# A seven-bank PSUM ring as one tensor, with two neighbouring banks read by one instruction

## Chip, cores and metric

The kernel runs on one core of a Trainium2 chip. The metric is the device time in microseconds (us) of one execution. The kernel before took 1364.9 us (median of three runs, 1364.61 to 1367.81). The profiled execution took 1365.17 us, and its span, from the first to the last instruction, is 1363.4 us.

## What is computed

One decoder layer in fp32 on x of shape (4, 1024, 256) with a context of shape (4, 64, 256): self-attention, cross-attention and a ternary feed-forward, each behind a layer norm and added to x.

```python
x = x + attn(layernorm(x), W_qkv, b_qkv, W_out, b_out)       # 16 heads of 16, softmax(q k) / 16
x = x + xattn(layernorm(x), ctx, Wq, bq, Wk, bk, Wv, bv, Wo, bo)
x = x + ffn(layernorm(x), W_fc, ln_w, ln_b, W_proj)          # 256 -> 1024 -> 256, gelu, layernorm
```

Self-attention is most of the work: 4 batches x 16 heads x 1024 x 1024 scores, which are computed twice, once to find the row maxima and once, transposed, to take the exponential.

## The kernel before

**Units and steps.** The scores are worked in 16 units `u` (a batch and a group of four heads, two pairs of two). A unit has 16 steps (`half`, `kb`): a block of 128 keys against 512 queries, in the loop at lines 891 to 956. There are thus 256 steps. In each step TensorE gets, in program order (`ordered` at lines 54 to 63 fixes the order of TensorE and of the DMA queue, not that of the readers):

1. `scores(..., 0)` (L872): a product for each of two heads into two banks of PSUM, then a second product that subtracts the maxima (`sel`, `mT`). The two heads sit in the two halves of TensorE's rows, so the products of a pair run side by side. ScalarE then takes Exp of each bank (L888).
2. `top()`: the next piece of `maxima` (L412) for the unit after: two more banks of scores, which VectorE reduces to a row maximum, one bank at a time (L433).
3. Perhaps a filler ("rows": a turning of blocks by TensorE transposes into two banks, or a piece of cross-attention in two banks).
4. `scores(..., 1)`: two banks. 5. `top()`: two banks.
6. `weigh` (L796): the exponentials of the step before, times the values, into the one bank `ps_acc`.
7. Perhaps fillers ("cols": a projection or the like, one bank each).

**The ring.** PSUM has eight banks here, of 512 fp32 columns in 128 partitions. One is `ps_acc`; seven are a pool `ps_ring` (L175), handed out in turn by `bank()` (L183), so the n-th allocation gets the bank of the (n-7)-th. The first product into a bank waits for the instruction that last read it. `two_banks()` (L186) hands out two banks in a row. The fillers are chosen in `fill` (L692) by credits and due times when the program is built; nothing of that choice depends on how a bank is read.

**Readers of two banks.** Besides L433 and L888, two banks are filled together and read by two instructions in `turned` (L200: the copies at L269, L307, L451 and L604, and the reciprocal and product of `normalised`, L298 and L299), at L592 (maxima of cross-attention) and at L625 (its exponentials). After the last unit the ring is closed (L962) and the feed-forward runs with two other pools, `ps_wide` and `ps_misc`, which the change does not touch in size.

Of the kernel before, what the change touches and what calls it, by code (L numbers as in the profile page):

```python
# [30 lines left out]
def decoder_layer(ctx, tc, a, out):  # L31
# [23 lines left out]

    def matmul(*args, **kwargs):
        ordered(nc.tensor.matmul(*args, **kwargs))  # L57

    def transpose(*args):
        ordered(nc.tensor.transpose(*args))  # L60
# [68 lines left out]
    nc.vector.memset(eps_t, LN_EPS)  # L129
# [45 lines left out]
    open_psum("ring", 7, [P, 512])  # L175
# [10 lines left out]
    def two_banks():  # L186
        return [bank() for _ in range(2)]
# [12 lines left out]
    def turned(blocks):  # L200


        n = len(blocks)
        sides = 2 if state["split"] else 1
        w = P // sides
        banks = [bank() for _ in range(sides)]
        for i, block in enumerate(blocks):
            for r, pt in enumerate(banks):
                side = slice(w * r, w * r + w)
                transpose(pt[:, i * w : (i + 1) * w], block[side, :], ident[side, side])  # L210
        return [pt[:, 0 : n * w].rearrange("p (b i) -> p b i", i=w) for pt in banks]

    def turned_tokens(copy, src, n):


        step = min(n, 4) if state["split"] else 2
        for k0 in range(0, n, step):
            sides = turned([src(c, k0 + k) for c in range(2) for k in range(step)])
            for r, v in enumerate(sides):
                copy(  # L220
                    slice(k0 * P, (k0 + step) * P), r, len(sides),
                    v.rearrange("p (c k) i -> p c k i", c=2),
                )

    def of_side(dst, r, sides):

        return dst.rearrange("p c (k r i) -> p r c k i", r=sides, i=P // sides)[:, r, :, :, :]

    def ln_stats(pool, mv, blocks):

        for i, t in blocks:
            st = pool.tile([P, 6], F32, tag="bn", name="bn", bufs=3)
            nc.vector.bn_stats(out=st, in_=xs(t)[:, 0, :])  # L233
            nc.vector.bn_aggr(out=mv[:, i, :], in_=st)

    def ln_rstd(pool, rs, mv):
        n = mv.shape[1]
        sd = pool.tile([P, n], F32, tag="sd", name="sd", bufs=2)
        nc.scalar.activation(sd, mv[:, :, 1], AF.Sqrt, bias=eps_t[:, 0:1])
        nc.vector.reciprocal(out=rs, in_=sd)  # L240

    def ln_normalised(pool, mv, rs, i, t, n):
        xn = pool.tile([P, n, E], F32, tag="xn", name="xn", bufs=2)
        if state["split"]:
            nmr = pool.tile([P, n], F32, tag="nmr", name="nmr", bufs=2)
            nc.vector.scalar_tensor_tensor(
                nmr, mv[:, i : i + n, 0], -1.0, rs[:, i : i + n], ALU.mult, ALU.mult
            )
            for k in range(n):
                nc.scalar.activation(  # L250
                    xn[:, k, :], xs(t + k)[:, 0, :], AF.Identity, bias=nmr[:, k : k + 1],
                    scale=rs[:, i + k : i + k + 1],
                )
            return xn
        for k in range(n):
            nc.vector.tensor_scalar(  # L256
# [5 lines left out]
    def ln_transposed(dst, xn, rest=None):  # L262

        def copy(tokens, r, sides, v):
            to = of_side(dst[:, :, tokens], r, sides)
            nc.scalar.copy(to, v)  # L269
            if rest is not None:  # L270
                nc.vector.tensor_tensor(  # L271
                    of_side(rest[:, :, tokens], r, sides), v, to.bitcast(F32), ALU.subtract
                )

        turned_tokens(copy, lambda c, k: xn[:, k, c * P : (c + 1) * P], xn.shape[1])
# [9 lines left out]
    def head_proj(dst, w, bias, g, src, cols):  # L285
        pq = bank()[:, 0 : cols.stop - cols.start]
        product(pq, [(w[:, c, g * P : (g + 1) * P], src[:, c, cols]) for c in range(2)])
        nc.scalar.activation(dst[:, cols], pq, AF.Identity, bias=bias[:, g : g + 1])

    def normalised(dst, acc_sb):  # L290


        views = turned([acc_sb[:, n * P : (n + 1) * P] for n in range(4)])
        n = NG // len(views)
        for side, v in enumerate(views):
            heads = v.rearrange("p t (j e) -> p t j e", e=32)
            r = post_pool.tile([P, 4, n, 1], F32, tag="r", name="r", bufs=3)
            nc.vector.reciprocal(out=r, in_=heads[:, :, :, 0:1])  # L298
            nc.vector.tensor_tensor(  # L299
                dst[:, :, side * n : (side + 1) * n, :], heads[:, :, :, 1 : 1 + D],  # L300
                r.to_broadcast([P, 4, n, D]), ALU.mult,
            )

    def transposed_blocks(src, n):
        t = post_pool.tile([P, 2, n * P], F32, tag="ao", name="ao")
        turned_tokens(
            lambda tokens, r, sides, v: nc.scalar.copy(of_side(t[:, :, tokens], r, sides), v), src, n  # L307
        )
        return t

    def out_proj(ao, k, n, w, t):
# [5 lines left out]
        nc.vector.tensor_tensor(  # L317
# [23 lines left out]
    def project(b, c):  # L341
# [6 lines left out]
        for side, half in ((0, 0), (1, 0), (1, 1), (0, 1)):  # L348
# [3 lines left out]
            for i0 in range(0, 512, width):  # L352
# [6 lines left out]
                nc.scalar.activation(hl[:, 0, part].bitcast(F32R), pq, AF.Identity, bias=bias)  # L359
                nc.vector.scalar_tensor_tensor(  # L360
# [40 lines left out]
    def values(b):  # L401
        for i in range(NT):
# [4 lines left out]
            nc.scalar.copy(  # L407
# [4 lines left out]
    def maxima(u):  # L412
# [4 lines left out]
        for half in range(2):  # L417
# [4 lines left out]
            for t, pair in order:  # L422
                q, k = qk_of[u][pair]
                for kh in range(2):
                    sides = two_banks()
# [6 lines left out]
                    for n, pm in enumerate(sides):  # L432
                        nc.vector.tensor_reduce(  # L433
                            mx[:, t, 2 * pair + n : 2 * pair + n + 1, kh], pm, AX.X, ALU.max
# [5 lines left out]
    def turn_maxima(u, mx):  # L440
        nm = main.tile([P, 4, NG], F32, tag="nm", name="nm", bufs=2)
        nc.vector.tensor_reduce(nm, mx, AX.X, ALU.max, negate=True)
        by_side = nm.rearrange("p t (a n) -> p t n a", a=2)
        dst = nm_s[:, :, :, 0:2, :]
        nc.vector.tensor_copy(dst[:, :, :, :, 0].bitcast(F32R), by_side)
        nc.vector.tensor_tensor(dst[:, :, :, :, 1], by_side, dst[:, :, :, :, 0], ALU.subtract)
        yield
        views = turned([nm_s[:, n, :, :, :].rearrange("p n a l -> p (n a l)") for n in range(4)])
        mT = main.tile([P, 512], F32R, tag="mT", name="mT", bufs=3)
        for r, v in enumerate(views):  # L450
            nc.scalar.copy(mT.rearrange("p (k r i) -> p r k i", r=len(views), k=4)[:, r, :, :], v)  # L451
# [27 lines left out]
    def context():  # L479
# [9 lines left out]
        nc.vector.tensor_reduce(own, ident.rearrange("p (s j i) -> p j s i", s=2, j=4), AX.XY, ALU.add)  # L489
        one = post_pool.tile([P, 32], F32, tag="one", name="one")  # L490
        nc.vector.tensor_reduce(one, ident.rearrange("p (s h l) -> p h s l", s=2, l=2), AX.XY, ALU.add)
        nc.vector.tensor_copy(
            sel_x, one[:, 0:8].rearrange("p (h o) -> p h o", o=1).to_broadcast([P, 8, SK])
        )
        for c in range(2):
# [5 lines left out]
            for j in range(4):  # L501
                nc.vector.tensor_scalar(
# [3 lines left out]
        for b in range(B):  # L506
# [9 lines left out]
            for n in range(2):  # L516
                r = slice(64 * n, 64 * n + 64)
                nc.vector.tensor_tensor(
# [5 lines left out]
    def value_bias():  # L524
# [10 lines left out]
        nc.vector.scalar_tensor_tensor(bo, pt, 1.0 / 16.0, bo, ALU.mult, ALU.add)  # L535
# [4 lines left out]
    def post(b):  # L540
# [25 lines left out]
        for half in range(2):  # L566
# [6 lines left out]
            ln_transposed(xnT, xn)  # L573
# [7 lines left out]
            for t in range(4):  # L581
                yield "rows"
                pm = two_banks()
# [7 lines left out]
                for s in range(2):  # L591
                    nc.vector.tensor_reduce(  # L592
                        nm[:, t, s, :], pm[s].rearrange("p (h k) -> p h k", k=SK), AX.X, ALU.max,
# [4 lines left out]
            nc.vector.tensor_copy(dst[:, :, :, :, 0].bitcast(F32R), nm)  # L598
            nc.vector.tensor_tensor(dst[:, :, :, :, 1], nm, dst[:, :, :, :, 0], ALU.subtract)
            yield "rows"  # L600
            views = turned([nm_x[:, t, :, :, :].rearrange("p s h l -> p (s h l)") for t in range(4)])
            mT = post_pool.tile([P, 512], F32R, tag="mTx", name="mTx")
            for r, v in enumerate(views):
                nc.scalar.copy(mT.rearrange("p (k r i) -> p r k i", r=len(views), k=4)[:, r, :, :], v)  # L604
            att = post_pool.tile([P, 4, NG, NG * D], F32, tag="attx", name="attx")
            before = None
            for g in range(NG):
                yield "rows+" if g else "rows"
                pe = two_banks()
# [14 lines left out]
                for p in range(2):  # L624
                    nc.scalar.activation(ex[:, p, :], pe[p], AF.Exp, scale=0.25)  # L625
# [11 lines left out]
                nc.scalar.copy(oT, pa)  # L637
# [84 lines left out]
    def ternary(name, *shape):  # L722
# [13 lines left out]
        for i, cols in enumerate(parts):  # L736
            yield "free"
            nc.vector.tensor_reduce(
# [3 lines left out]
        nc.vector.memset(ones, 1.0)  # L742
# [4 lines left out]
        nc.vector.tensor_reduce(thr[:, 0:1], pt[:, 0 : len(parts)], AX.X, ALU.add)  # L747
        nc.vector.tensor_scalar(thr[:, 0:1], thr[:, 0:1], 1.0 / (P * n), GAMMA_EPS, ALU.mult, ALU.add)
        nc.vector.tensor_scalar(thr[:, 1:2], thr[:, 0:1], -0.5, None, ALU.mult)
        nc.vector.tensor_scalar(thr[:, 0:1], thr[:, 0:1], 0.5, None, ALU.mult)  # L750
        for cols in parts:
            yield "free"
            neg = main.tile([P, 512], F32, tag="hl", name="neg", bufs=2)
            nc.vector.tensor_scalar(neg, flat[:, cols], thr[:, 1:2], None, ALU.is_lt)
            nc.vector.scalar_tensor_tensor(
# [4 lines left out]
    def bias_row():  # L760
# [10 lines left out]
        nc.vector.tensor_copy(yrow, pt[:, 0:E])  # L771
# [24 lines left out]
    def weigh(u, half, kb, exps, acc):  # L796
# [11 lines left out]
        nc.scalar.copy(oT, acc)  # L808
# [27 lines left out]
    for pair in range(2):  # L836

        for n in range(2):
            c = 64 * n + 2 * pair
            for i in range(2):  # L840
                nc.vector.tensor_tensor(
                    sel_f[:, pair, :], sel_f[:, pair, :], ident[:, c + i : c + i + 1].to_broadcast([P, P]), ALU.add
                )
    nc.vector.tensor_copy(sel, sel_f)
# [27 lines left out]
    def scores(u, half, kb, pair):  # L872

        q, k = qk_of[u][pair]
        pe = two_banks()
# [11 lines left out]
        for n in range(2):  # L887
            nc.scalar.activation(ex[:, n, :], pe[n], AF.Exp)  # L888
# [74 lines left out]
    main_stack.close()  # L963
    open_psum("wide", 2, [P, 2, 512])
# [11 lines left out]
    def widen(i):  # L976
# [3 lines left out]
        for t in range(0, NH, 2):  # L980
            cols = slice(t * P, (t + 2) * P)
            xn = ln_normalised(ffn, mv3, rs3, t0 + t, t0 + t, 2)
            ln_transposed(xh[:, :, cols], xn, rest=xl[:, :, cols])
# [7 lines left out]
        for t in range(NH):  # L991
# [9 lines left out]
            nc.scalar.activation(h[:, t, :], ph.rearrange("p a f -> p (a f)"), AF.Gelu)  # L1001
            st = ffn.tile([P, 2, 6], F32, tag="bnh", name="bnh", bufs=3)
            for half in range(2):
                nc.vector.bn_stats(out=st[:, half, :], in_=h[:, t, half * 512 : (half + 1) * 512])  # L1004
            nc.vector.bn_aggr(out=mv[:, t, :], in_=st)
# [3 lines left out]
        nc.vector.scalar_tensor_tensor(nmr, mv[:, :, 0], -1.0, rs, ALU.mult, ALU.mult)  # L1009
        for t in range(0, NH, 2):  # L1010
            yield ""
            nc.vector.tensor_scalar(
                h[:, t, :], h[:, t, :], mv[:, t, 0:1], rs[:, t : t + 1], ALU.subtract, ALU.mult
            )
            nc.scalar.activation(
# [4 lines left out]
    def narrow(i):  # L1020
# [6 lines left out]
        for c in range(HID // P + 2):  # L1027
            if c < HID // P:
# [6 lines left out]
                nc.scalar.activation(hT, pt, AF.Copy, scale=w)  # L1035
                nc.vector.scalar_tensor_tensor(hl, pt, w, hT.bitcast(F32), ALU.mult, ALU.subtract)  # L1036
# [13 lines left out]
        for n in range(2):  # L1050
            rows = xs(t0 + 2 * n, 2)
            nc.vector.tensor_tensor(
# [111 lines left out]
```

## Time and profile before

| view | value |
|---|---|
| time, three runs | 1364.9 us (1364.61 to 1367.81) |
| profiled execution: time, span, mean granted clock | 1365.17 us, 1363.4 us, 0.979 |
| stage with the ring: the 256 steps | from 58 us to 1098 us |
| TensorE busy, 60 to 340 / 340 to 640 / 640 to 1000 us | 267.36 / 294.17 / 352.89 us |
| VectorE busy in the same stretches | 211.24 / 237.91 / 283.13 us |
| ScalarE busy in the same stretches | 191.54 / 214.13 / 252.76 us |
| feed-forward and last cross-attention, 1100 to 1363 us: TensorE, VectorE, ScalarE busy | 235.04 / 170.29 / 157.53 us |

The groups in the profile have the line, engine and operation, what is written and read with partitions x elements, the count, the time that at least one of them was busy, the mean duration of one, and the idle time of the engine before them with what ended it. PE is TensorE's products, PEld its weight loads, DVE is VectorE, ACT ScalarE. All products have line 57 and all transposes line 60, since one helper each records them; what they are is told by the tiles: `ps_ring<-q,k` is a product of `scores`, `ps_ring<-mT,sel` its second product, `ps_ring<-k,q` one of `maxima`, `ps_acc<-exp,v_sb` one of `weigh`.

### The profile page before, as it was taken

How to read it: one execution, taken by the hardware profiler on the slowest of the kernel's cores; microseconds unless marked ns; L12 is line 12 of the kernel's file. 1: busy time of each engine (PE TensorE's matmuls, PEld its weight loads, DVE VectorE, ACT ScalarE, POOL GpSimd, SP SyncE). 2: the span in 40 equal slices, each digit the busy share in tenths (PEclk: the TensorE clock that was granted, in tenths of full speed). 3: DMA queues.
4: the chain of work that ended last, by engine and by line, in shares of the span. 5: the costliest groups of instructions: out<-in, count | busy, mean ns of one | idle time of the engine just before them, and what ended most of it. 6: DMA issues, size and time to landing. Idle time of an engine off the chain costs nothing.

```text
span 1363.4 us, 27651 instructions
## 1 busy us (share of the span) xinstructions
PE 1282.1 (94%) x11000; PEld 717.4 (53%) x11000; DVE 1004.7 (74%) x2110; ACT 898.5 (66%) x1654; POOL 80.0 (6%) x86
## 2 busy tenths in 40 slices
PE   3879999999999999999999999999999988999987
PEld 1434445545545454444545544545455466776777
DVE  4877777867878877877877777878889357565665
ACT  1377666756687667777676676676766746474765
POOL 4000000003010000011000000010000012000000
PEclk9889999999999999989999999999999989999989
DMA  5440312312130202131212112212210010100000
GB/s 169 126 143 30 111 42 68 94 48 63 41 85 1 63 7 57 33 93 31 64 35 60 38 27 75 82 53 73 55 40 1 2 62 1 44 19 31 1 31 32
DMA packets 46064, 72.72 MB, mean 53 GB/s; under 512 B 11280, under 2 KB 27920, under 8 KB 45936
## 3 DMA queue, kind: packets, MB, share of 16 engines
q1 hardware_dynamic: 44720, 68.47, 17.0%
q8 instruction: 87, 1.43, 0.4%
q10 hardware_dynamic: 1072, 2.10, 0.4%
q0 software_dynamic: 144, 0.39, 0.2%
q14 instruction: 41, 0.34, 0.1%
HBM read 46.81 MB, written 24.12 MB: 52 GB/s over the span
## 4 chain that ended last, share of the span: by engine, by line
PE 73%; DVE 16%; ACT 8%; issue 2%; DMA 1%; SPq 0%; DVEq 0%; ACTq 0%
PE ps_ring L57 42%; PE ps_acc L57 15%; PE ps_wide L57 8%; DVE mx L433 8%; PE ps_misc L57 3%; ACT exp L888 3%; PE ps_misc L60 2%; PE ps_ring L60 2%; DVE nm L592 2%; ACT xn L250 1%; DVE xn L256 1%; DVE bn L233 1%; DMA x<-in_x 1%; ACT ex L625 1%; ACT hl L359 1%
## 5 line engine op out<-in xcount | busy, mean ns | idle before, releaser
L433 DVE TENSOR_REDUCE mx<-ps_ring 128x1 f32<-128x512 f32 x1024 | 646.4, 682 | 157.6 <-PE ps_ring L57 156.7
L888 ACT ACTIVATE exp<-ps_ring 128x512 f32<-128x512 f32 x1024 | 549.2, 606 | 191.1 <-PE ps_ring L57 187.5
L57 PE MATMUL ps_ring<-q,k 64*128 64x512 f32 x1024 | 280.5, 474 | 8.0 <-ACT exp L888 5.9
L57 PE MATMUL ps_ring<-k,q 64*128 64x512 f32 x1024 | 260.2, 425 | 20.1 <-DMA q<-kept_q 7.9
L57 PE MATMUL ps_acc<-exp,v_sb 128*32 128x512 f32 x2048 | 275.3, 610 | 0.0
L57 PE MATMUL ps_ring<-mT,sel 64*128 64x512 f32 x1024 | 232.8, 400 | 0.2 <-ACT mT L451 0.2
L57 PEld LDWEIGHTS ps_ring<-q,k 64*128 64x128 f32 x1024 | 115.5, 185 | 198.4 <-ACT exp L888 69.0
L57 PEld LDWEIGHTS ps_ring<-k,q 64*128 64x128 f32 x1024 | 124.2, 186 | 100.2 <-ACT exp L888 41.3
L57 PEld LDWEIGHTS ps_ring<-mT,sel 64*128 64x128 f32 x1024 | 108.0, 186 | 6.3 <-ACT mT L451 0.7
L57 PEld LDWEIGHTS ps_acc<-exp,v_sb 128*32 128x32 f32 x2048 | 40.5, 108 | 67.4 <-issue 65.6
L1004 DVE BATCH_NORM_STATS2 bnh<-h 128x6 f32<-128x512 f32 x64 | 41.2, 679 | 34.1 <-ACT h L1001 34.0
L1001 ACT ACTIVATE h<-ps_wide 128x1024 f32<-128x1024 f32 x32 | 32.7, 1026 | 41.6 <-PE ps_wide L57 41.5
L1036 DVE SCALAR_TENSOR_TENSOR hl<-ps_misc,lnw,hT 128x512 fp32r<-128x512 f32 x64 | 46.4, 733 | 18.2 <-ACT hT L1035 18.2
L57 PE MATMUL ps_wide<-wproj,hl 128*128 128x256 f32 x256 | 46.2, 303 | 12.6 <-DVE hl L1036 12.5
L57 PE MATMUL ps_wide<-wfc,xl 128*128 128x512 f32 x128 | 56.5, 442 | 1.4 <-DVE xl L271 1.4
L57 PE MATMUL ps_wide<-wfc,xh 128*128 128x512 f32 x128 | 54.3, 424 | 0.0
L1035 ACT ACTIVATE hT<-ps_misc,lnw 128x512 fp32r<-128x512 f32 x64 | 42.6, 687 | 16.3 <-PE ps_misc L60 16.3
L233 DVE BATCH_NORM_STATS2 bn<-x 128x6 f32<-128x256 f32 x96 | 38.8, 416 | 8.1 <-DMA x<-in_x 6.4
L57 PEld LDWEIGHTS ps_wide<-wproj,hl 128*128 128x128 f32 x256 | 34.9, 191 | 16.2 <-DVE hl L1036 14.8
L280 POOL TENSOR_TENSOR x<-x,xbo 128x512 f32<-128x512 f32 x16 | 20.6, 1295 | 367.0 <-ACT xn L250 358.5
L57 PE MATMUL ps_wide<-wproj,hT 128*128 128x256 f32 x256 | 41.4, 284 | 0.0
L407 ACT COPY v_sb<-ps_ring 128x256 f32<-128x256 f32 x32 | 12.0, 375 | 41.0 <-PE ps_ring L57 30.6
(166 smaller groups left out, 1467.1 us busy)
## 6 DMA issues: line engine op xcount, KB each, us to landing
k<-kept_k SPq DMA_DIRECT2D x248, 64.0 KB
q<-kept_q SPq DMA_DIRECT2D x240, 64.0 KB
kept_q<-hl SPq DMA_DIRECT2D x15, 512.0 KB
kept_k<-hl SPq DMA_DIRECT2D x14, 512.0 KB
out<-x SPq DMA_DIRECT2D x16, 256.0 KB
x<-in_x SPq DMA_DIRECT2D x3, 1024.0 KB
x_kept<-x SPq DMA_DIRECT2D x3, 1024.0 KB
x<-x_kept SPq DMA_DIRECT2D x3, 1024.0 KB
```

The lines of the kernel that those rows point to most:

```text
L57: ordered(nc.tensor.matmul(*args, **kwargs))
L60: ordered(nc.tensor.transpose(*args))
L233: nc.vector.bn_stats(out=st, in_=xs(t)[:, 0, :])
L250: nc.scalar.activation(xn[:, k, :], xs(t + k)[:, 0, :], AF.Identity, bias=nmr[:, k : k + 1], scale=rs[:, i + k : i + k + 1],)
L280: nc.gpsimd.tensor_tensor(xs(t, 2), xs(t, 2), row.rearrange("p (o d) -> p o d", o=1).to_broadcast([P, 2, E]), ALU.add,)
L433: nc.vector.tensor_reduce(mx[:, t, 2 * pair + n : 2 * pair + n + 1, kh], pm, AX.X, ALU.max)
L592: nc.vector.tensor_reduce(nm[:, t, s, :], pm[s].rearrange("p (h k) -> p h k", k=SK), AX.X, ALU.max, negate=True,)
L888: nc.scalar.activation(ex[:, n, :], pe[n], AF.Exp)
L1001: nc.scalar.activation(h[:, t, :], ph.rearrange("p a f -> p (a f)"), AF.Gelu)
L1004: nc.vector.bn_stats(out=st[:, half, :], in_=h[:, t, half * 512 : (half + 1) * 512])
L1035: nc.scalar.activation(hT, pt, AF.Copy, scale=w)
L1036: nc.vector.scalar_tensor_tensor(hl, pt, w, hT.bitcast(F32), ALU.mult, ALU.subtract)
```

## The change

The seven banks become one tensor `ring` of 128 x 7 x 512, allocated once; `ring_bank()` hands its banks out in the same order as before. As all instructions on it now touch one tensor, each is told by hand which others it need not wait for: an instruction names the span of banks that it touches, and is freed of those that touch other banks only (`by_bank`, called for each instruction of TensorE, VectorE and ScalarE through a thin wrapper). `two_banks()` returns beside the two banks a list of views: one view of both when they are neighbours in the tensor, and two views of one bank each when the first is bank 6 and the second bank 0. The readers loop over the views, so two neighbouring banks are read by one instruction. The order of TensorE's instructions is unchanged.

```diff
+    NB = 7
+    rings = []
+    spans = [(i, i + n) for n in (1, 2) for i in range(NB + 1 - n)]
+    def by_bank(ins, *operands):
...
+                at = ap.offset % (NB * 512)
+                last = at + sum(step * (count - 1) for step, count in ap.ap[1:])
+                mine = at // 512, last // 512 + 1
...
+            for span in spans:
+                if span[1] <= mine[0] or mine[1] <= span[0]:
+                    tc.add_to_no_dep_group(f"not_{span}", ins.ins)
+            tc.declare_no_dep(ins.ins, group=f"not_{mine}", keep=keep, reason="other banks")
...
-    open_psum("ring", 7, [P, 512])
+    ring = ring_pool.tile([P, NB, 512], F32, name="ps_ring")
+    def ring_bank():
+        i = ring_at[0]
+        ring_at[0] = (i + 1) % NB
+        return ring[:, i, :]
...
     def two_banks():
-        return [bank() for _ in range(2)]
+        i = ring_at[0] if state["banks"] == "ring" else NB
+        pair = [bank() for _ in range(2)]
+        if i + 1 < NB:
+            return pair, [(slice(0, 2), ring[:, i : i + 2, :])]
+        return pair, [
+            (slice(n, n + 1), one.rearrange("p (o f) -> p o f", o=1)) for n, one in enumerate(pair)
+        ]
...
-                    for n, pm in enumerate(sides):
-                        nc.vector.tensor_reduce(
-                            mx[:, t, 2 * pair + n : 2 * pair + n + 1, kh], pm, AX.X, ALU.max
+                    for n, v in views:
+                        vector.tensor_reduce(
+                            mx[:, t, 2 * pair + n.start : 2 * pair + n.stop, kh], v, AX.X, ALU.max
                         )
...
-        for n in range(2):
-            nc.scalar.activation(ex[:, n, :], pe[n], AF.Exp)
+        for n, v in views:
+            scalar.activation(ex[:, n, :], v, AF.Exp)
         return ex
```

The same loop over views is put at L269, L307, L451, L604, L298 and L299, L592 and L625. In `normalised` the transposes write their 64 columns as two runs of 32, so that the heads of both banks lie in one regular pattern for the reader.

## Prediction, written before the changed kernel was run

> **What bounds the kernel now.** I read the page first, for busy time and the two big readers of the ring, then the waits, then the timeline of single steps.
>
> ```profile
> PE 1282.1 (94%) x11000; PEld 717.4 (53%) x11000; DVE 1004.7 (74%) x2110; ACT 898.5 (66%) x1654; POOL 80.0 (6%) x86
> ...
> L433 DVE TENSOR_REDUCE mx<-ps_ring 128x1 f32<-128x512 f32 x1024 | 646.4, 682 | 157.6 <-PE ps_ring L57 156.7
> L888 ACT ACTIVATE exp<-ps_ring 128x512 f32<-128x512 f32 x1024 | 549.2, 606 | 191.1 <-PE ps_ring L57 187.5
> ```
>
> TensorE sets the pace; VectorE and ScalarE are idle a quarter and a third of the time, waiting for TensorE's products. But 94% does not mean that TensorE is never held up: its records are modelled, and a product that started late still looks busy. The waits of its weight loads from 60 to 1098 us say more (in total, how many, the longest):
>
> ```profile
> PEld ps_ring L57 <- ACT exp L888: 113.4, 310, 1.7
> ...
> PEld ps_ring L57 <- DVE mx L433: 41.3, 90, 1.6
> ```
>
> 310 loads wait for an Exp and 90 for a maximum: TensorE wants a bank that its last reader has not given back. Which reader of a pair it is, the timeline shows. A step without filler, 2.90 us long (columns: start, length, engine, what, count, idle before and who ended it):
>
> ```profile
> 109.49 0.50 PE L57 MATMUL ps_ring<-q,k 64*128 64x512 f32 x2
> ...
> 110.32 2.07 ACT L888 ACTIVATE exp<-ps_ring 128x512 f32<-128x512 f32 x4 [1.06 <-PE ps_ring L57]
> 110.49 2.48 DVE L433 TENSOR_REDUCE mx<-ps_ring 128x1 f32<-128x512 f32 x4 [0.27 <-PE ps_ring L57]
> ...
> 110.75 0.71 PE L57 MATMUL ps_ring<-k,q 64*128 64x512 f32 x2
> 110.97 0.18 PEld L57 LDWEIGHTS ps_ring<-k,q 64*128 64x128 f32 x1 [0.26 <-ACT exp L888]
> ...
> 111.39 1.06 PE L57 MATMUL ps_acc<-exp,v_sb 128*32 128x512 f32 x8
> 112.39 0.19 PEld L57 LDWEIGHTS ps_ring<-q,k 64*128 64x128 f32 x2 [0.84 <-ACT exp L888]
> ```
>
> Count the banks of this step: scores 0, 1; maxima 2, 3; scores 4, 5; maxima 6, 7. Bank 7 of seven is bank 0 again, which this step's own first Exp reads. That Exp starts at 110.32, ends 0.60 later at 110.92, and the load for the eighth product starts at 110.97. Its partner started at 110.75, so TensorE has lost 0.22 us already, and what follows is late by that.
>
> I counted this over the whole ring, by giving each bank in TensorE's order its last reader and comparing that reader's end with the first load of the bank's next use, seven places on. In 505 places of 2575 the load comes no later than 0.13 us after the reader's end. In 268 of these the reader is the first of a pair, in 184 the second, in 53 a single one; 96 and 95 of the first kind are the second score product or the second maximum behind the first Exp. So the release that TensorE stands and waits for is mostly that of a first bank, which one instruction over both banks delays.
>
> **The change, part by part.** *The readers' cost.* The nearest row to an Exp of 1024 is the Gelu over two banks at L1001, 1026 ns, against 606 ns for the Exp of 512. Four chained Exps take 2.07 us, so a second one adds 0.49 us: the pair ends now 1.09 us after its start, in future 1.03. A maximum takes 682 ns; the additions at L317 take 415 ns for 256 elements and 676 for 512, thus 0.52 us per 512, and a maximum over 1024 about 0.68 + 0.53 = 1.21 us, where the pair ends now after 1.29. Saved per merged pair: 0.06 us of ScalarE, 0.08 of VectorE. Following the bank numbers modulo seven, 1013 of 1190 pairs become one instruction (444 of 512 of Exp, 432 of 512 of maxima); the others straddle banks 6 and 0. That is 27 us of ScalarE and 35 of VectorE, all beside TensorE's work: both engines already wait for products.
>
> Here the Trainium skill speaks for a larger gain: "ScalarE: Activation LUTs", in "What ACT_TABLE_LOAD costs", gives an ACTIVATE 186 ns apart from its elements, and "Advanced Engine Details and Errata", "The Read-Write Bubble", advises 512 or 1024 elements to spread such a cost. With 186 ns the saving would be 83 us of ScalarE; the chain of four shows that most of it overlaps already, and I take 0.06. Either number is off TensorE's path.
>
> *The releases.* The first bank of a merged pair comes back at 1.03 us instead of 0.60 (+0.43) behind an Exp and at 1.21 instead of 0.68 (+0.53) behind a maximum. In the step above: reader 110.32 + 1.03 = 111.35, load at 111.40 instead of 110.97, and `ps_acc` and the next step follow 0.43 later. Nothing hides it: TensorE runs in order, the products behind it wait too, and the wait begins anew in each step from that step's first scores, so it adds up step by step instead of being paid once. The products of the next step find their banks long free (the second pair of Exps ends at about 1.9 + 0.9 us into a step that then lasts 3.3).
>
> A step with turned blocks has ten banks, and the second score product is the one that takes bank 0 again:
>
> ```profile
> 1061.44 1.08 ACT L888 ACTIVATE exp<-ps_ring 128x512 f32<-128x512 f32 x2 [0.45 <-PE ps_ring L57]
> ...
> 1062.09 0.18 PEld L57 LDWEIGHTS ps_ring<-q,k 64*128 64x128 f32 x1 [0.23 <-ACT exp L888]
> ...
> 1062.57 0.19 PEld L57 LDWEIGHTS ps_ring<-k,q 64*128 64x128 f32 x2 [0.19 <-ACT exp L888]
> ...
> 1063.01 1.07 PE L57 MATMUL ps_acc<-exp,v_sb 128*32 128x512 f32 x8
> ```
>
> Now two waits follow each other, on the first Exp (1062.03) and on the second (1062.52). Merged, both banks come at 1062.47: the second score product loads at 1062.52, the second product of that side runs 0.23 later, the last maximum another 0.23 later at 1062.98, when its bank is free as well (this step's maxima start at 1061.68; + 1.21). `ps_acc` starts 0.43 after that, as it does now after 1062.58: 1063.41 instead of 1063.01, +0.40. The same working for a step that turns the maxima (at 610.02 us) gives +0.28; I take +0.36 for the mixture. If the first pair straddles the ring's end, the merged maxima still bind here, so no share is taken off.
>
> With 16 steps of cross-attention's maxima (at 504.84) the same sums give +0.35, and with its exponentials (at 536.23) +0.02, since there the product that takes bank 0 starts at 1.90 us anyway.
>
> *The sum.* I sorted the 256 steps by their order of products:
>
> - 103 with nothing or only column fillers between: 0.43 x 219/256 (the share of first score pairs that are neighbours) x 103 = 38 us
> - 84 with one turning: 0.36 x 84 = 30 us
> - 24 with cross-attention's maxima: 8 us; 10 with two turnings, at the same 0.35: 4 us; 22 with its exponentials: under 1 us
> - 13 odd ones: not costed
>
> Together +80 us in 1040 us of steps. Against it stands about 1 us before the first step, where 22 maxima run back to back on VectorE (13.25 us from 40.57). The feed-forward stage has other pools and one-bank views, so the same instructions; the transposes' runs of 32 columns I put at nothing: the whole of the turnings of `normalised` is 25.6 us of products, most beside other work, so even a tenth more is under 3 us. The profiled run took 1365.2 us, 1.8 beyond its span; 1365.2 + 80 = 1445, and the median of the runs lies only 0.3 lower.
>
> The skill has a rule against the change too: "Perfetto Trace Analysis", "Matmuls" under "Optimizing Tensor Performance", wants product groups to rotate through banks so that reading one overlaps the next group's products. Seven banks read singly rotate; read in twos, the ring holds three and a half. It gives no price; the 0.43 us above is this trace's.
>
> **Rivals.** *Partly hidden, 1403.* The turning steps have two waits in a row and readers that are late for other reasons (a maximum there starts only when VectorE has finished a row of small operations), so that the quicker pairs give back what the later first bank takes. Then only the 103 plain steps pay: 1365 + 38. Against it stand the two workings above, +0.40 and +0.28.
>
> *Faster, 1350.* If the second bank of a pair is what holds TensorE, merging helps: it comes 0.06 to 0.08 us sooner. 184 such places give 12 us, and VectorE's and ScalarE's links in the chain that ended last (maxima 8%, Exp 3% of the span, about 150 us, at 6%) another 8 at most, overlapping: some 15 us. This decides only if fewer than about 28 of the 268 first-bank waits are felt (28 x 0.43 = 12). For it speaks that both readers are busy two thirds of the time and more; against it, that the waits sit at the first Exp.
>
> *The waits are not by the bank, about 2000.* If a product waited for all earlier readers of the one tensor, each of four pairs in a step would pay a reader of 1.0 to 1.2 us: at least 2.5 us in each of 256 steps. The spans in the diff name disjoint banks one by one, so I hold it unlikely.
>
> **Chances.** As worked 0.72 (1425 to 1470), partly hidden 0.13, faster 0.07, no change 0.03 (both effects small), waits too wide 0.05. The range from 1400 to 1475 holds the first two but for their edges. A difference of 0.3%, 4 us, is about what measurement can tell from none: faster 0.07, within it 0.03, slower 0.90.
>
> **What would show it.** Right: Exp of 1024 at 1.03 us and maxima of 1024 at 1.21, about 512 + 68 of each; the plain step at 3.33 us instead of 2.90, with the load of its eighth product 1.9 us after its start; waits for Exp longer in total by most of 80 us; TensorE's granted clock and its durations unchanged. Wrong: plain steps of 2.90 us, or a merged reader that costs as much as two, or loads that wait for readers of banks they do not write.

## The result, and the profile after

The changed kernel takes 1452.2 us (median of four runs, 1450.58 to 1454.93) against 1365.7 us (four runs, 1364.61 to 1367.81): a ratio of 1.0633, 95% interval 1.0612 to 1.0655. It is 86.5 us slower, where 80 were forecast. The profiled execution took 1454.93 us, with a span of 1453.2 us and a mean granted clock of 0.973.

Every instruction of the three engines now carries L110, the line of the wrapper that records it, so readers are told by tiles and shapes. The first fence is the page's line of busy time, the second the groups with shapes kept apart.

```profile
PE 1315.1 (91%) x11000; PEld 720.5 (50%) x11000; DVE 988.4 (68%) x1563; ACT 873.1 (60%) x1144; POOL 79.8 (5%) x86
```

```profile
L110 DVE TENSOR_REDUCE mx<-ps_ring 128x2 f32<-128x1024 f32 x432 | 524.3, 1220 | 197.8 <-PE ps_ring L110 196.6
L110 ACT ACTIVATE exp<-ps_ring 128x1024 f32<-128x1024 f32 x444 | 447.0, 1024 | 224.8 <-PE ps_ring L110 221.8
...
L110 DVE TENSOR_REDUCE mx<-ps_ring 128x1 f32<-128x512 f32 x160 | 103.0, 682 | 26.2 <-PE ps_ring L110 26.2
...
L110 ACT ACTIVATE exp<-ps_ring 128x512 f32<-128x512 f32 x136 | 73.8, 596 | 29.0 <-PE ps_ring L110 28.1
```

A merged Exp takes 1.02 us and a merged maximum 1.22. There are 444 and 432 of them, and 2 x 68 and 2 x 80 single ones where a pair straddles the ring's end. VectorE lost 547 instructions and 16 us of busy time, ScalarE 510 and 25 us. The two engines did get less to do; the span still grew by 90 us.

The plain step shown for before, in the timeline of after, 3.34 us long instead of 2.90:

```profile
114.13 0.50 PE L110 MATMUL ps_ring<-q,k 64*128 64x512 f32 x2
...
114.97 2.00 ACT L110 ACTIVATE exp<-ps_ring 128x1024 f32<-128x1024 f32 x3 [1.24 <-PE ps_ring L110]
...
116.04 0.18 PEld L110 LDWEIGHTS ps_ring<-k,q 64*128 64x128 f32 x1 [0.69 <-ACT exp L110]
...
116.47 1.07 PE L110 MATMUL ps_acc<-exp,v_sb 128*32 128x512 f32 x8
...
117.47 0.19 PEld L110 LDWEIGHTS ps_ring<-q,k 64*128 64x128 f32 x2 [0.84 <-issue]
```

The Exp begins 0.84 us after the step's start, as it did (0.83). The merged Exp ends at about 114.97 + 1.02 = 115.99, and the eighth product's load starts at 116.04: 1.91 us into the step where it was 1.48. `ps_acc` and the next step follow, 0.44 us later than before. The next lines show the turning step (1061.44 in the prediction's fence), now 4.61 us long instead of 4.19:

```profile
1149.31 1.02 ACT L110 ACTIVATE exp<-ps_ring 128x1024 f32<-128x1024 f32 x1 [0.52 <-PE ps_ring L110]
...
1150.39 0.18 PEld L110 LDWEIGHTS ps_ring<-q,k 64*128 64x128 f32 x1 [0.67 <-ACT exp L110]
...
1150.85 0.18 PEld L110 LDWEIGHTS ps_ring<-k,q 64*128 64x128 f32 x1 [0.17 <-DVE mx L110]
...
1151.29 1.06 PE L110 MATMUL ps_acc<-exp,v_sb 128*32 128x512 f32 x8
```

First the second score product waits for the merged Exp, then the last maximum for a merged maximum. `ps_acc` starts 2.75 us into the step instead of 2.34: +0.41.

The waits from 60 to 1190 us, in total, how many, the longest:

```profile
PEld ps_ring L110 <- issue: 244.5, 584, 1.7
PEld ps_ring L110 <- ACT exp L110: 136.6, 229, 3.2
...
PE ps_ring L110 <- ACT exp L110: 60.8, 162, 2.9
...
PEld ps_ring L110 <- DVE mx L110: 30.3, 70, 0.8
```

For Exp the loads waited 113.4 us before and the products 8.0; now 136.6 and 60.8, in fewer and longer waits (a product and its load may show the same wait). "Issue" grew from 143.1 to 244.5, but much of that is a change of name: the 0.84 us ahead of the next step's first load (117.47 above) was put down to an Exp before (112.39 in the prediction) and is put down to issue now. Of the 310 loads that before shows behind an Exp, 43 are such ones of about 0.84 us, 36 of the 113.4 us in all; in after they are 3. The prediction read them as waits for a bank too. Without them, what the loads wait for Exp rose from 77 to 134 us. In the chain that ended last, Exp rose from 3% to 12% of the span, and TensorE fell from 73% to 69%.

### The profile page after: what moved, and what is told of

Same layout as the page of the kernel before. It is cut to its first block, busy times and chain, and to the rows that moved or that the text cites. A ratio compares the mean times of both kernels' runs of the same rounds, so it can differ in the third digit from the quotient of the medians.

```text
span 1453.2 us, 26471 instructions
## 1 busy us (share of the span) xinstructions
PE 1315.1 (91%) x11000; PEld 720.5 (50%) x11000; DVE 988.4 (68%) x1563; ACT 873.1 (60%) x1144; POOL 79.8 (5%) x86
## 4 chain that ended last, share of the span: by engine, by line
PE 69%; ACT 16%; DVE 10%; issue 2%; DMA 2%; ACTq 0%; SPq 0%; DVEq 0%
PE ps_ring L110 40%; PE ps_acc L110 16%; ACT exp L110 12%; PE ps_wide L110 8%; PE ps_misc L110 5%; DVE mx L110 4%; DVE nm L110 1%; DMA x<-in_x 1%; DVE hl L110 1%; ACT L110 1%; ACT xn L110 1%; DVE xn L110 1%; DVE bn L110 0%; ACT h L110 0%; ACT hl L110 0%
## 5 line engine op out<-in xcount | busy, mean ns | idle before, releaser
L110 DVE TENSOR_REDUCE mx<-ps_ring 128x2 f32<-128x1024 f32 (+1 forms) x592 | 625.1, 1075 | 224.0 <-PE ps_ring L110 222.8
L110 ACT ACTIVATE exp<-ps_ring 128x1024 f32<-128x1024 f32 (+1 forms) x580 | 517.3, 924 | 253.8 <-PE ps_ring L110 249.9
L110 PE MATMUL ps_ring<-k,q 64*128 64x512 f32 x1024 | 292.7, 416 | 54.3 <-ACT exp L110 32.9
L110 PE MATMUL ps_ring<-q,k 64*128 64x512 f32 x1024 | 299.5, 475 | 28.8 <-ACT exp L110 22.6
L110 PE MATMUL ps_acc<-exp,v_sb 128*32 128x512 f32 x2048 | 280.0, 618 | 0.0
L110 PE MATMUL ps_ring<-mT,sel 64*128 64x512 f32 x1024 | 246.3, 406 | 0.1
L110 PEld LDWEIGHTS ps_ring<-q,k 64*128 64x128 f32 x1024 | 123.7, 186 | 232.5 <-issue 136.2
L110 PEld LDWEIGHTS ps_ring<-k,q 64*128 64x128 f32 x1024 | 142.7, 187 | 142.2 <-ACT exp L110 73.5
L110 PEld LDWEIGHTS ps_ring<-mT,sel 64*128 64x128 f32 x1024 | 113.2, 187 | 5.5 <-ACT mT L110 0.6
L110 PEld LDWEIGHTS ps_acc<-exp,v_sb 128*32 128x32 f32 x2048 | 40.8, 109 | 71.7 <-issue 62.2
L110 DVE BATCH_NORM_STATS2 bnh<-h 128x6 f32<-128x512 f32 x64 | 41.2, 679 | 34.6 <-ACT h L110 34.5
L110 DVE SCALAR_TENSOR_TENSOR hl<-ps_misc,lnw,hT 128x512 fp32r<-128x512 f32 x64 | 46.4, 733 | 18.2 <-ACT hT L110 18.2
L110 PE MATMUL ps_wide<-wfc,xl 128*128 128x512 f32 x128 | 56.9, 445 | 1.4 <-DVE xl L110 1.4
L110 ACT ACTIVATE h<-ps_wide 128x1024 f32<-128x1024 f32 x32 | 32.7, 1026 | 41.8 <-PE ps_wide L110 41.6
L110 PE MATMUL ps_wide<-wproj,hl 128*128 128x256 f32 x256 | 46.0, 302 | 12.6 <-DVE hl L110 12.5
L110 PE MATMUL ps_wide<-wfc,xh 128*128 128x512 f32 x128 | 54.8, 428 | 0.0
L110 ACT ACTIVATE hT<-ps_misc,lnw 128x512 fp32r<-128x512 f32 x64 | 42.7, 687 | 16.3 <-PE ps_misc L110 16.3
L110 DVE BATCH_NORM_STATS2 bn<-x 128x6 f32<-128x256 f32 x96 | 38.8, 417 | 9.4 <-DMA x<-in_x 7.6
L110 DVE SCALAR_TENSOR_TENSOR hl<-ps_ring,bq_c,hl 128x256 f32<-128x256 f32 (+1 forms) x30 | 15.0, 501 | 43.0 <-ACT hl L110 41.8
L110 PEld LDWEIGHTS ps_wide<-wproj,hl 128*128 128x128 f32 x256 | 34.7, 190 | 16.2 <-DVE hl L110 14.8
```

Of the source, the lines that this page charges most:

```text
L110: ins = make(*args, **kwargs)
```

## Experiments

Theory: the 86 us are the late release of a pair's first bank, step by step. First rival: they come from the seven banks being one tensor, with waits told by hand. Second rival: from what the waits do to TensorE's clock or to the order of the readers. "After" and "before" in the short diffs are the two kernels.

**One tensor, nothing merged** (from after):

```diff
-    def two_banks():
+    def two_banks(merge=False):
...
-        if i + 1 < NB:
+        if merge and i + 1 < NB:
```

> The change with its one tensor and its waits by the bank, but two banks are never read by one instruction. Late-release theory (a merged reader gives back the first of its two banks 0.43 to 0.53 us later, and TensorE waits for that bank once in most steps): the cost is gone, about 1366 us, within 10 us of the kernel before. Rival (the single tensor, its waits or the readers' changed order cost the time): 1440 us or more, as with the change whole. Plain steps: 2.90 and 3.77 us by the first theory, 3.33 and 4.20 by the rival.

Measured: 1383.3 us, ratio 1.0139 (1.0124 to 1.0154). Neither end: 17.6 us are there without any merging. The median plain step is as before (2.90 us, and 3.77 with a column filler, in both), so the 17.6 us are no cost per step: they lie in some nine places (steps 5, 7, 21, 38, 53, 76, 130, 140, 204), each a stall that before did not have. The other 69 us of the change belong to merging.

**Only the Exps merged, and only the maxima merged** (from the kernel of the first experiment; `two_banks(True)` in `scores` alone, or in `maxima` alone):

```diff
-        pe, views = two_banks()
+        pe, views = two_banks(True)
```

> One tensor; only the two Exps of a pair of scores are merged, all other pairs are read singly. Late-release theory: the first Exp's bank is the one awaited in plain steps (+0.43) and in steps with a turning (+0.4), so nearly the whole cost is here: +75 to +85 us, 1440 to 1450. Rival (cost spread over all merged readers by their number): 444 of 1013 merged pairs, so +38 us, about 1404.

> One tensor; only the two maxima of a pair are merged, all other pairs are read singly. Late-release theory: no plain step waits for a maximum's first bank, so they stay at 2.90 and 3.77 us; steps with a turning or with cross-attention's maxima wait for it last: +0.36 in 84 and +0.3 in 24, times 6 in 7: about +32 us, 1397. So merged maxima and merged Exps together cost less than their sum. Rival (spread by number): 432 of 1013, +37 us, about 1402, but in plain steps as much as in others.

Measured: 1441.2 us (1.0551, 1.0535 to 1.0567) and 1403.1 us (1.0275, 1.0260 to 1.0290). Over the single tensor that is 57.8 us for Exp and 19.8 for the maxima; both together cost 68.9. That the two levels come near those expected (1440 to 1450, and 1397) is in part luck: they had been counted from 1366, and the 17.6 us of the ring stand in for what the parts fall short. They do not add up because in a turning step either alone is worth most of the delay: the median of those with one turning and a column filler rises by 0.41 us with Exp alone, by 0.34 with maxima alone, and by 0.41 with both. Plain steps rise by 0.43 with Exp merged and by nothing with maxima merged.

**Only the second pair's Exps merged** (from the first experiment):

```diff
-        pe, views = two_banks()
+        pe, views = two_banks(pair == 1)
```

> One tensor; only the Exps of the second pair of scores in a step are merged, all else is read singly. Late-release theory: the first bank of that pair is wanted by the next step's maxima at the earliest, over 1 us after even the merged Exp has ended, so nothing is lost, and nothing gained either, since ScalarE is not on the path: the 1383 us of the single readers on one tensor, within 6 us. Rival (each merged instruction costs its share): 221 of 1013 pairs of the 69 us that merging costs, +15 us, 1398.

Measured: 1380.0 us (1.0107, 1.0083 to 1.0130), 3.3 us under the single tensor's time, and the two intervals overlap. Its 225 merged Exps cost nothing where no product waits for their first bank, so it is not the merged instruction that is dear: it is the first score pair's release.

**The same late release without merging.** First try, in before:

```diff
-        for n in range(2):
+        for n in (1, 0):
```

> The kernel before with seven tiles and all readers single; only the two Exps of a pair are taken in reverse order, second bank first. Nothing is merged and the work is the same. Late-release theory: the first bank comes back 1.09 us after the pair's start instead of 0.60, +0.49 in plain steps, which no straddling pair spares, +0.4 in steps with a turning: +50 and +35 and +14, about 1464 us. Rival (merging, the single tensor or the longer instruction itself costs): no change, 1366 us.

Measured: 1366.0 us (1.0002, 0.9993 to 1.0011). It tells nothing: the readers' order is planned anew when the program is built, and in the built program 486 of the 512 pairs stood in their old order (the median plain step is 2.90 us as before). Second try, from the first experiment, with the order of these instructions held:

```diff
-        for n, v in views:
-            scalar.activation(ex[:, n, :], v, AF.Exp)
+        for n, v in reversed(views):
+            ordered(scalar.activation(ex[:, n, :], v, AF.Exp))
```

> One tensor, banks in fixed turn, all readers single; the two Exps of a pair are held in reverse order, second bank first. No instruction is merged, added or longer. Late-release theory: the first bank is given back at 1.09 us instead of 0.60, later still than by a merged Exp (1.03): +0.49 us in 103 plain steps, +0.4 in 84 with a turning, some in 34 others, 85 to 100 us on top of 1383: 1468 to 1483. Rival (the long instruction itself or its waits cost the time): 1383.

Measured: 1459.8 us (1.0684, 1.0660 to 1.0709), 76.5 us over the single tensor with every Exp still 512 long. The same plain step, 3.40 us long:

```profile
111.05 2.07 ACT L110 ACTIVATE exp<-ps_ring 128x512 f32<-128x512 f32 x4 [0.81 <-PE ps_ring L110]
...
112.18 0.18 PEld L110 LDWEIGHTS ps_ring<-k,q 64*128 64x128 f32 x1 [0.75 <-ACT exp L110]
...
112.60 0.16 PEld L110 LDWEIGHTS ps_acc<-exp,v_sb 128*32 128x32 f32 x8 [0.24 <-issue]
```

The first bank is read second, and the eighth product's load comes 1.13 us after the first Exp's start, where merged it was 1.07. Plain steps rise by 0.50 us, those whose pair straddles the ring's end too (merging leaves these alone). Delaying a release alone makes the loss; merging is only one way to delay it. No run held the Exps in their usual order, so what the holding does by itself is not measured; but no step grew by more than 1.7 us, and some of the single tensor's stalls are gone (steps 5, 7, 21, 38 and 53 are 2.6 to 3.5 us shorter), so the loss is the rise of the ordinary steps. The time is a little below the range expected, the mechanism as expected.

**Where the 17.6 us come from.** In the built kernel before, the pool of seven does not hand out its banks in turn: in 496 of 2575 allocations the bank is not the one of seven places back, since the plan made at build time takes the bank that it sees free first. The single tensor goes round strictly. First, the recorded sequence of before was handed out in the single tensor (from the first experiment, `HANDED` being the 2582 recorded banks):

```diff
-        i = ring_at[0]
-        ring_at[0] = (i + 1) % NB
+        i = int(HANDED[ring_at[0]])
+        ring_at[0] += 1
```

> One tensor, waits by the bank, all readers single, but the banks are handed out in the very sequence that the pool of seven tiles gave them in the kernel before (it takes the bank that the plan at build time sees free first, which in 496 of 2575 cases is not the bank of seven places back). If the fixed turn of the banks is what costs 17.5 us with single readers, the time returns to 1366 us, within 5. If the waits of the one tensor or the readers' changed order cost them, it stays at 1383.

Measured: 1376.9 us (1.0086, 1.0067 to 1.0104): 6.5 us given back, 11 left. Then the reverse, before with seven ordinary tiles in a fixed turn:

```diff
-    open_psum("ring", 7, [P, 512])
+    for i in range(7):
+        open_psum(f"ring{i}", 1, [P, 512])
...
+        turn[0] = (i + 1) % 7
+        return ps[f"ring{i}"]()
```

> The kernel before with its seven ring banks as seven pools of one tile each, handed out in fixed turn; every bank is read alone, and no wait is told by hand. If the 17.5 us that the single tensor costs without merging (1383.3) come from the fixed turn and from the readers' order that is planned with it, about 1383 us. If they come from the single tensor and its waits, the time stays at 1366. Handing out the old sequence of banks in the single tensor gave back 6.5 us, which would leave 1372 as the time if the turn alone counts for what it did there.

Measured: 1382.0 us (1.0129, 1.0109 to 1.0148), the single tensor's time within the intervals, with stalls in nearly the same steps. So the tensor and its hand-told waits cost nothing that can be measured, and the fixed turn, with the plan that goes with it, accounts for the 17 us. One of these steps, first in before, 4.06 us long, then with tiles in fixed turn, 8.10 us:

```profile
631.12 1.28 ACT L239 ACT_TABLE_LOAD   x1
...
632.26 0.18 PEld L57 LDWEIGHTS ps_ring<-k,q 64*128 64x128 f32 x1 [0.41 <-DVE mx L433]
...
632.69 1.06 PE L57 MATMUL ps_acc<-exp,v_sb 128*32 128x512 f32 x8
632.73 1.28 ACT L888 ACT_TABLE_LOAD   x1
...
634.02 1.57 ACT L888 ACTIVATE exp<-ps_ring 128x512 f32<-128x512 f32 x3
```

```profile
643.18 1.28 ACT L248 ACT_TABLE_LOAD   x1
...
644.79 1.28 ACT L897 ACT_TABLE_LOAD   x1
...
646.09 2.06 ACT L897 ACTIVATE exp<-ps_ring 128x512 f32<-128x512 f32 x4
646.73 0.18 PEld L57 LDWEIGHTS ps_ring<-k,q 64*128 64x128 f32 x1 [2.82 <-ACT exp L897]
646.74 0.59 PE L57 MATMUL ps_ring<-k,q 64*128 64x512 f32 x1 [2.51 <-ACT exp L897]
...
647.26 1.93 PE L57 MATMUL ps_acc<-exp,v_sb 128*32 128x512 f32 x8
```

In both ScalarE loads tables for a square root and for Exp again, and its first Exp starts 3.5 us into the step, where 0.8 is usual. Before, the eighth product has the bank of a maximum, free at 632.21, and `ps_acc` runs while the Exps are still to come. In fixed turn it has bank 0 and waits 2.5 us for the late Exp. After that TensorE's granted clock is down, as three windows of the second kernel show (columns: from and to, length, busy time and instructions of PE, PEld, DVE, ACT and POOL, then PEclk, DMA share and GB/s):

```profile
641.50:646.70 5.20, 2.73 (x35) 1.43 (x23) 3.58 (x11) 3.95 (x6) 0.00 (x0) 1.00 0.00 0
646.70:650.60 3.90, 3.86 (x25) 1.17 (x25) 0.69 (x1) 2.42 (x5) 1.27 (x1) 0.56 0.00 0
650.60:655.00 4.40, 4.40 (x35) 2.43 (x31) 3.16 (x6) 4.20 (x9) 1.29 (x1) 1.00 0.30 119
```

The eight products into `ps_acc` take 1.93 us instead of 1.06. The stall and its clock cost 4.0 us in this one step.

**Moving `weigh` ahead of the product that waits** (in before, the second `top()` put behind `weigh` and its fillers):

```diff
-            for _ in range(2 if u == 0 and step < 3 else 1):
-                top()
...
+            for _ in range(2 if u == 0 and step < 3 else 1):
+                top()
```

> The kernel before with one edit in TensorE's order: weigh and the column fillers come before the second call of top, so the last maximum of a step, whose second product waits for the first Exp's bank, comes a microsecond later. By the late-release theory that wait (0.22 us in plain steps) falls away where a column filler stands between: 76 x 0.21 + 27 x 0.06, about 18 us faster, 1347; steps with a turning keep theirs, since their second score product waits. If the waits were not what TensorE loses there, no change, 1366.

Measured: 1407.7 us (1.0309, 1.0289 to 1.0329), a miss. The waits for Exp did shrink, but others took their place (compare 113.4, 41.3 and, for transposes at L60 behind a maximum, 3.1 us before):

```profile
PEld ps_acc L57 <- issue: 89.9, 246, 0.7
PEld ps_ring L57 <- DVE mx L433: 74.5, 182, 1.1
PEld ps_ring L57 <- ACT exp L888: 64.1, 99, 1.5
PEld ps_ring L60 <- DVE mx L433: 35.3, 89, 1.5
```

The maxima now come late in the step, and the next step's products and transposes wait for them: by the median, a plain step grows by 0.04 us, a turning step by 0.14, one with cross-attention's pieces by 0.34.

**The readers in program order.** To take the planned order of the readers out of the comparison, VectorE's and ScalarE's instructions were held in program order, in the single tensor, in before, and in after (the diff is that of the two tensor kernels; before got a wrapper that does the same):

```diff
                 ins = make(*args, **kwargs)
+                if self.engine is not nc.tensor:
+                    ordered(ins)
```

> One tensor, banks in fixed turn, all readers single, and VectorE's and ScalarE's instructions held in the order in which the program names them, as TensorE's are. If the 17.5 us that the single readers cost on one tensor come from readers that the plan at build time put in an order that does not fit the fixed turn (the step at 155.6 us: a projection's reader behind four Exps holds the bank that the last maxima need, TensorE stands 2.4 us and then runs at half clock for 3.4 us), most of them go: 1366 to 1372 us. If the one tensor's waits cost them, it stays at 1383.

> The kernel before with its pool of seven tiles, and VectorE's and ScalarE's instructions held in the order in which the program names them. The control for the run above: in the kernel before the pool gives each product the bank that comes free first, so an odd order of readers costs little; no change to a few us faster, 1357 to 1366 us.

> The change whole (two neighbouring banks read by one instruction), with VectorE's and ScalarE's instructions held in program order. If merging and the readers' order are two separate costs, the 69 us of merging stay and only the other part goes: 69 us over the same kernel with single readers held in order, 1435 to 1441 us. If the order of the readers is what the merged kernel suffers from, it falls below 1400.

Measured: 1457.8 us (1.0671, 1.0648 to 1.0693), 1440.3 us (1.0552, 1.0530 to 1.0574) and 1516.2 us (1.1096, 1.1078 to 1.1113). All three levels were missed, by 75 to 92 us: program order is far worse for all three. Only 22 to 27 us of each loss lie in the 256 steps, where the median plain step is untouched (2.90 to 2.91 us in both unmerged ones) and single steps stall by 2 to 6 us. The larger part lies behind them, where the ring is no longer used: from its last use to the end it is 259 us in the three kernels with the planned order, and 298 to 304 in these. So these runs say less of the ring than their times suggest. But the differences stand: merging costs 58 us here by the medians, and 69 us in the profiles' 256 steps (73 with the planned order), and the single tensor 17.5 us over before, as with the planned order.

## Why the prediction was right, and where it was not

*The readers' cost.* Right: 1.02 and 1.22 us where 1.03 and 1.21 were worked out, and the counts exactly. The busy time of all Exps fell by 28 us (549.2 to 447.0 + 73.8) for 27 forecast, that of the maxima by only 19 (646.4 to 524.3 + 103.0) for 35: the forecast set a merged maximum against a pair of 1.29 us, but many pairs followed each other, and four chained maxima took 2.48 us already. What ScalarE and VectorE saved gained nothing: the kernel with only second pairs merged stays at the single tensor's time.

*The releases.* Right, and shown by three runs: Exps merged in both pairs cost 58 us, in second pairs alone nothing, and a late release without merging 76 us. The Trainium skill, in "Perfetto Trace Analysis" under "Optimizing Scalar/DVE Operations", has the rule that fits: where these engines are not saturated but make others wait, breaking instructions up can let work end sooner. It gives no price; here merging cost 68.9 us while the engines were 68% and 60% busy.

*The sum.* The steps of the single tensor and of after, one against the other in their profiles, by the kinds of the prediction:

| kind of step | forecast, us | measured, us |
|---|---|---|
| plain (103) | 38 | 34.1 |
| one turning (84) | 30 | 27.9 |
| cross-attention's maxima (forecast 24, here 18) | 8 | 5.8 |
| two turnings, or one with maxima (forecast 10, here 16) | 4 | 2.2 |
| cross-attention's exponentials | under 1 | 1.3 |
| odd ones (12 or 13) | not costed | 1.6 |
| all | 80 | 73.0 |

A typical step was right (plain with a neighbouring first pair +0.435 us for 0.43; turning +0.41 for 0.40 and 0.36; plain with a straddling pair 0.00). The sum is 7 too high in the profiles, 11 by the medians of the runs (68.9), because each kind was costed as if all its steps were typical: some steps gave less or nothing (steps 5, 53, 129 and 131, near the single tensor's stalls, even became 1.0 to 1.7 us shorter).

*The step that failed* is the statement in the section on the change that the banks come "in the same order as before", on which the prediction's count by sevens rests. The pool does not go round; it sidesteps a bank whose reader is late. Giving that up cost 17.6 us that no part of the sum names. It fell on the same side as the overestimate of merging, and so it is luck that the total came within 7 us; two errors of 11 and 17.6 us stand behind that.

*"TensorE's granted clock unchanged"* was wrong. In the 256 steps, apart from a stretch of 6.8 us at their start that all these kernels have, before spent 17 us at half clock, after 37.5. Half clock about halves what TensorE does (1.93 us for 1.06 in the step above), so these 20 us more are worth at most 10 of the 86 (an estimate). In the single tensor without merging it was 37.5 us as well, with the tiles in fixed turn 34, so this loss came with the long stalls of the fixed turn and not with merging.

*The rivals.* Partly hidden (1403) fell: turning steps pay 0.41 us. Faster (1350) fell: the second bank's earlier release shows nowhere. Waits wider than a bank (about 2000) fell: the single tensor unmerged equals the tiles in the same turn.

*Open.* Why before's sequence of banks gave back only 6.5 of 17.6 us in the single tensor: three long stalls remained (steps 7, 53 and 130, 3 to 4 us each). That sequence had been chosen together with an order of the readers, which the build plans anew; no run separated the two. Which reader must stand ahead of which, so that program order loses 64 to 75 us, in the steps and more so behind them, was not tried one by one either. No version tried was faster than before.

## To carry to other kernels

Before two reads of a buffer are made one, look for who waits for the first half: the price is its later release, paid again in each round in which a product stands at that buffer, and the saving counts only if the reader's engine is the bound. Merge where nobody waits (here the second pair), and take a delayed release without merging as the control. When a pool becomes one hand-run ring, check in the built program whether the pool really went round: an allocation that takes what comes free first hides a late reader, and a fixed turn does not.

## What the hardware showed

A long stall of TensorE can cost more than its length: in the step above, 2.5 us of it became 4.0. In the profile of after, from 60 us on, TensorE stood idle for 2 us or more 12 times (2.1 to 3.6 us), and each time a stretch of half clock, 3.4 or 6.8 us long, began between 1.8 us before and 1.6 us after the idle time's end; of five idle stretches of 1.4 to 1.6 us, one was followed so. With the tiles in fixed turn it was 10 of 12. The many waits of half a microsecond in plain steps left the clock at 1.00 (from 410 to 630 us, for example). The Trainium skill, in "TensorE: Matmul & The Clock Gate" under "What's actually happening", speaks of an idle window of about 3.4 us; here 2.1 us of idle time were enough.
